# Twenty-four products of a constant on TensorE between two layers of a fused kernel

## The chip, the cores and the metric

The kernel runs on one core of a Trainium2 chip. A core has five engines with a queue of instructions each: TensorE (PE; its weight loads are listed as PEld), VectorE (DVE), ScalarE (ACT), GpSimd (POOL) and SyncE (SP), which here only issues transfers. An engine takes its instructions in the order of its queue and waits on semaphores for the others. The metric is the device time of one execution in microseconds, as the median of several runs.

## The reference

Two transformer layers over 8 sequences of 256 tokens with 256 features, all in float32:

```python
x = x + attention_0(layernorm(x))      # softmax over rows plus softmax over columns, 16 heads
x = x + experts_0(layernorm(x))        # 4 experts, top 2 of them, and one shared expert for all tokens
x = x + time_mixing_1(layernorm(x))    # RWKV: a recurrence over time, then a norm, a gate and a product
x = x + experts_1(layernorm(x))        # 8 experts, top 2 of them, with biases
```

The shared expert is `(silu(xt @ sw1.T) * (xt @ sw3.T)) @ sw2.T`. The time mixing makes three mixtures of each token with the one before it, multiplies each by a 256x256 matrix (k, v and r), and runs the recurrence over k and v.

## The kernel before

Everything stays in on-chip memory as `xs[b]`, one tile per sequence. The experts work on gathered rows: for each layer the sequences are split in two groups (five and three), so there are four expert objects: `one` and `two` for the first layer, `three` and `four` for the second. Each writes its normed tokens to DRAM (`asked`), chooses and routes them, gathers them back in tiles of 128 rows of one expert each (`xg`, L1002, an indirect transfer issued by POOL), turns each tile on TensorE (L1012), multiplies it by the expert's weights (L1020), and scatters the results (L1050). `combine` adds them to `xs[b]` (L1111).

The handoff between the layers is where the second group still has shared-expert work (`two.shared()`, L941 to L954), the time mixing of earlier sequences is under way, and `three`'s tiles begin. The time mixing of one sequence is ten stages: `norm` (L216 and L217 on POOL, L235 on ScalarE: xr), `mix` (transposes L246, the copy L1151, VectorE's dx L1141 and the mixtures L1159), `project` (24 products L1170, copies L1178 and L1176), `exponents` (L1186, L1141 with d, then L1196 to L1200 on ScalarE), `denominator` (L1209), `invert` (L1217), `numerator` (L1224), `norm_inner` (transposes L1236, statistics L1241), `gate` and `project_out`.

Three things set the order of the work. The generators are woven together in Python (`weave`), which gives the order in which instructions are written down. A planner then places them: it models the time, and at each point takes the ready instruction with the highest precedence, which is the order of writing, changed by `tc.high_priority(offset=n)` (a positive n puts a block ahead, a negative one behind). Third, `tc.issue_after(i)` says that what the block issues on the engine of instruction i must be queued behind i. The result is a fixed queue for each engine. PSUM tiles come from tags with a number of buffers: in this part `mm` has three, `ps` two, `sc` three. The shared expert and the tiles' products (L1020) take theirs from `mm`.

The second layer's expert weights (`v1s`, `v2s`, L1345 to L1347) are fetched during the handoff as well, into the place of the first layer's weights. `ones` is a constant 128x128 tile of float32 that is filled at the start.

The lines that the change follows, at the handoff:

```python
with tc.issue_after(three.routed.ins):
    weave((shared, 4))          # the rest of two.shared()
ctx0.close()
...
weave((back, 3), (take(mixing, 3), 3))
tiles = three.tiles()
weave((take(behind(tiles, 3), 20), 20), (mixing, 15))
```

Of the kernel before, what the change touches and what calls it, by code (L numbers as in the profile page):

```python
# [17 lines left out]
P = 128  # L18
# [25 lines left out]
def weave(*streams):  # L44

    streams = [[g, n, 0] for g, n in streams]
    while streams:
        s = min(streams, key=lambda s: s[2] / s[1])
        s[2] += 1
        try:  # L50
            next(s[0])
        except StopIteration:
            streams.remove(s)
# [7 lines left out]
def take(gen, n):  # L61
    for _ in range(n):
        try:
            next(gen)
        except StopIteration:
            return
        yield
# [3 lines left out]
def two_layers(  # L71
# [26 lines left out]
    nc = tc.nc  # L98
# [25 lines left out]
    def filled(name, value, shape=(P, P)):  # L124
        t = const.tile(list(shape), F32, tag=name, name=name)
        nc.gpsimd.memset(t, value)
        return t

    ones = filled("ones", 1.0)
# [595 lines left out]
    class Experts:  # L725
# [206 lines left out]
        def shared(self):  # L932

            mm = self.mm
            for b in self.seqs:
                xt = self.xts[b]
                pu, pg = mm([P, HS // P, T]), mm([P, HS // P, T])
                for pp, w in ((pu, self.weights[3]), (pg, self.weights[4])):
                    for h in range(HS // P):
                        for c in range(NC):  # L940
                            nc.tensor.matmul(  # L941
                                pp[:, h, :], lhsT=w[:, c, ts(h, P)], rhs=xt[:, c, :], start=(c == 0), stop=(c == NC - 1)
                            )
                s = self.mp.tile([P, HS // P, T], F32, tag="h", name="hs", bufs=3)
                nc.scalar.activation(s, pu, AF.Silu)
                nc.vector.tensor_tensor(s, s, pg, ALU.mult)
                yield
                po = mm([P, TT, D])
                for t in range(TT):
                    for h in range(HS // P):  # L950
                        nc.tensor.matmul(
                            po[:, t, :], lhsT=s[:, h, ts(t, P)], rhs=self.weights[5][:, h, :], start=(h == 0), stop=(h == HS // P - 1)
                        )
                nc.vector.tensor_tensor(xs[b], xs[b], po, ALU.add)  # L954
                yield
# [394 lines left out]
    def layers(is_bounded):  # L1350
# [4 lines left out]
        with ExitStack() as pctx, ExitStack() as ctx0, ExitStack() as actx:  # L1355
# [7 lines left out]
            def bank(tag):  # L1363
                def fresh(shape):
                    return psum["pool"].tile(shape, F32, tag=tag, name=tag, bufs=psum[tag])

                return fresh

            mm, ps, sc = bank("mm"), bank("ps"), bank("sc")
            one, two = (Experts(0, k, w0, lnp, mp, rt, ps, mm, ps) for k in range(2))  # L1370
# [40 lines left out]
            def behind(gen, lag=1):  # L1411

                while True:
                    with tc.issue_after(on_pe[-lag].ins):
                        try:
                            next(gen)
                        except StopIteration:
                            return
                    yield

            steps = two.tiles()
            shared = two.shared()
            tiles = one_by_one(take(steps, 5), take(shared, 1), take(steps, 1), take(shared, 1), steps)
            weave((take(tiles, 1), 1))
            one.spare_tiles()
# [9 lines left out]
            with tc.issue_after(three.routed.ins):  # L1435
                weave((shared, 4))
# [5 lines left out]
            for m in (three, four):  # L1442
                m.weights, m.mp = w1_, mp
            weave((back, 3), (take(mixing, 3), 3))
            tiles = three.tiles()
            weave((take(behind(tiles, 3), 20), 20), (mixing, 15))
            assert four.chosen
# [34 lines left out]
    with tc.If(is_flat > 0) as which:  # L1482
        layers(True)
    with which.Else():
        attention_any()
        layers(False)
# [61 lines left out]
```

## Time and profile before

| | us |
|---|---|
| median of 3 runs (754.13 to 755.09) | 754.26 |
| the profiled execution | 760.07 |
| its span, first to last instruction | 757.7 |
| TensorE busy | 653.3 (86%) |
| VectorE busy | 462.9 (61%) |
| ScalarE busy | 358.8 (47%) |
| POOL busy | 244.5 (32%) |
| mean granted clock of TensorE | 0.941 |

A row of the timeline has the start and the duration in us, the engine, the line of the kernel, the operation with the tile written and the tiles read, the shape, and the number of instructions merged. A bracket at its end gives the idle time of the engine just before the row and what ended it. A row over a stretch of time gives the stretch, its length, TensorE's busy time and instructions in it, the clock granted to TensorE (1.00 is full), the busy share of the DMA engines and GB/s. In the rows by slices the span is cut in 40 equal parts and each digit is a share in tenths. A matmul's duration holds its way through the array, so that in a run of matmuls the next one starts well before the last one ends.

### The profile page before, as it was taken

To read this page: it belongs to the slowest core of one execution; us is meant where nothing else is said; L and a number is where in the kernel's file an instruction comes from. 1 tells how busy PE (TensorE), PEld (TensorE's weight loads), DVE (VectorE), ACT (ScalarE), POOL (GpSimd) and SP (SyncE) were. 2 spreads that over 40 slices of the span, in tenths; PEclk is the share of its full clock that TensorE was granted. 3 is DMA by queue.
4 is the path that set the end of the run, shared out by engine and by line. 5 is a ranking of instruction groups with operands and counts; after the bars stand their busy time and mean duration, and the time that the engine had idled before them with its cause. 6 is when DMAs were issued, how large, how long until landed. Compare 5 with 4: busy or idle time off the path is not lost. (4 is left out here: it accounts for less than half of the span.)

```text
span 757.7 us, 10756 instructions
## 1 busy us (share of the span) xinstructions
PE 653.3 (86%) x3170; PEld 417.3 (55%) x3170; DVE 462.9 (61%) x1216; ACT 358.8 (47%) x761; POOL 244.5 (32%) x319
## 2 busy tenths in 40 slices
PE   3799999996989999998899888986848989989790
PEld 2355555555765666665566656654735656554460
DVE  6699878897351111110866877673998895745542
ACT  3588767772213233322377467544147464423230
POOL 3434333300212333323222132112141446465430
PEclk9699999998999999999999999998879999999996
DMA  7800000001101111112300010002780445556844
GB/s 227 292 1 15 15 15 15 15 15 48 65 15 33 52 36 42 43 41 85 118 29 27 28 39 11 28 29 72 231 283 8 138 126 170 172 194 220 269 127 143
DMA packets 38547, 66.85 MB, mean 88 GB/s; under 512 B 6006, under 2 KB 20654, under 8 KB 38480
## 3 DMA queue, kind: packets, MB, share of 16 engines
q1 hardware_dynamic: 30400, 47.01, 18.9%
q0 software_dynamic: 7392, 18.50, 7.9%
q8 instruction: 31, 0.51, 0.3%
q10 hardware_dynamic: 688, 0.55, 0.2%
q14 instruction: 36, 0.29, 0.1%
HBM read 51.32 MB, written 16.41 MB: 89 GB/s over the span
## 5 line engine op out<-in xcount | busy, mean ns | idle before, releaser
L1002 POOL DMA_INDIRECT xg<-asked,source x77 | 78.4, 1018 | 186.5 <-PE ps L1012 164.1
L1050 POOL DMA_INDIRECT back<-yg,row_i x77 | 80.6, 1047 | 113.7 <-ACT yg L1049 35.3
L1041 DVE TENSOR_TENSOR h<-h,mm 128x512 f32<-128x512 f32 x37 | 25.3, 685 | 108.3 <-PE mm L1020 108.2
L1014 ACT COPY hT<-ps 128x256 f32<-128x256 f32 (+1 forms) x77 | 36.4, 473 | 95.8 <-PE ps L1012 87.2
L1020 PE MATMUL mm<-v1s,xgT 128*128 x160 | 76.9, 600 | 1.5 <-ACT xgT L1014 0.8
L576 ACT ACTIVATE e<-sc,minus 128x512 f32<-128x512 f32 x96 | 59.9, 711 | 28.5 <-PE sc L563 28.4
L1020 PE MATMUL mm<-w2s,hT 128*128 x296 | 72.0, 382 | 0.0
L1020 PE MATMUL mm<-w1s,xgT 128*128 x148 | 71.6, 602 | 0.2 <-ACT xgT L1014 0.2
L1020 PE MATMUL mm<-w3s,xgT 128*128 x148 | 70.7, 597 | 0.0
L577 DVE TENSOR_REDUCE s<-e 128x2 f32<-128x512 f32 x96 | 60.5, 677 | 13.3 <-ACT e L576 13.1
L563 PE MATMUL sc<-qT,kT 32*128 32x512 f32 x256 | 58.1, 703 | 2.9 <-DVE qT L544 2.2
L1020 PEld LDWEIGHTS mm<-w2s,hT 128*128 128x128 f32 x296 | 53.7, 191 | 7.1 <-issue 1.4
L1170 PE MATMUL sc<-mix,rw 128*128 128x256 f32 x192 | 49.3, 405 | 5.9 <-DVE mix L1159 4.2
L515 POOL TENSOR_TENSOR rr<-rr,minus_half 128x32 f32<-128x32 f32 x7 | 38.0, 5429 | 50.0 <-DVE rr L513 49.9
L1012 PEld LDWEIGHTS ps<-ident,h 128*128 128x128 f32 x228 | 28.8, 141 | 44.0 <-issue 27.7
L1020 PE MATMUL mm<-v2s,hT 128*128 x160 | 44.3, 396 | 3.1 <-ACT hT L1014 3.1
L216 POOL TENSOR_TENSOR rs<-mv,eps_ln 128x2 f32<-128x2 f32 x40 | 8.6, 215 | 118.4 <-DVE mv L211 75.6
L1012 PE MATMUL ps<-ident,h 128*128 128x128 f32 x228 | 39.4, 276 | 8.4 <-DVE h L1035 7.2
L1020 PEld LDWEIGHTS mm<-w3s,xgT 128*128 128x128 f32 x148 | 28.0, 193 | 33.9 <-issue 33.2
L1170 PEld LDWEIGHTS sc<-mix,rw 128*128 128x128 f32 x192 | 38.2, 205 | 14.2 <-DVE mix L1159 5.3
L1039 ACT ACTIVATE h<-mm 128x512 f32<-128x512 f32 x37 | 22.1, 598 | 43.1 <-PE mm L1020 43.1
L1032 DVE TENSOR_TENSOR hb<-mm,bias 128x512 f32<-128x512 f32 x40 | 27.5, 687 | 22.5 <-PE mm L1020 18.9
(246 smaller groups left out, 1254.2 us busy)
## 6 DMA issues: line engine op xcount, KB each, us to landing
bias<-bd SPq DMA_DIRECT2D x40, 384.0 KB
y<-back SPq DMA_DIRECT2D x16, 512.0 KB
asked<-xm SPq DMA_DIRECT2D x16, 256.0 KB
x<-in_x_dram SPq DMA_DIRECT2D x8, 256.0 KB
w1s<-in_w_dram SPq DMA_DIRECT2D x4, 512.0 KB
w3s<-in_w_dram SPq DMA_DIRECT2D x4, 512.0 KB
w2s<-in_w_dram SPq DMA_DIRECT2D x4, 512.0 KB
v1s<-in_v1g_dram SPq DMA_DIRECT2D x8, 256.0 KB
```

The costliest lines, as they stand in the source:

```text
L515: on_pool["last"] = nc.gpsimd.tensor_tensor(rr, rr, half, ALU.pow)
L563: nc.tensor.matmul(pa, lhsT=q["kT"][rows, u, ts(t, P)], rhs=q["qT"][rows, u], start=True, stop=True)
L576: nc.scalar.activation(e, pa, AF.Exp, bias=minus)
L577: nc.vector.tensor_reduce(q["s"][:, t, h : h + 2], e, AX.X, ALU.add)
L1002: nc.gpsimd.indirect_dma_start(out=xgs[j], out_offset=None, in_=self.asked, in_offset=bass.IndirectOffsetOnAxis(ap=self.source[:, j : j + ...
L1012: nc.tensor.transpose(pt[:, c, :], src[:, ts(c, P)], ident)
L1014: nc.scalar.copy(to, pt)
L1020: nc.tensor.matmul(po.unsqueeze(1), lhsT=lhsT[:, c, :], rhs=w[:, ds(e, 1), c, :], start=(c == 0), stop=(c == n - 1))
L1032: nc.vector.tensor_tensor(hb, ph, biases[j][:, 0 : 2 * I2], ALU.add)
L1041: nc.vector.tensor_tensor(s, s, pg, ALU.mult)
L1050: inst = nc.gpsimd.indirect_dma_start(out=self.back, out_offset=bass.IndirectOffsetOnAxis(ap=self.row[:, j : j + 1], axis=0), in_=yg, in_o ...
L1170: last = nc.tensor.matmul(po[:, o, :], lhsT=w[:, c, ts(o, P)], rhs=m[:, c, :], start=(c == 0), stop=(c == NC - 1))
```

## The change

It keeps a handle on the last product of the shared expert, and adds a block after the time-mixing steps that follow the weights' issue. The block opens a PSUM tile from tag `mm` and writes 24 products of `ones` with `ones` to it, each overwriting the last. All are to be queued on TensorE behind the last product of `two`'s shared expert, and their precedence is 400 places further back than where they are written. Nothing reads the tile.

```diff
@@ -948,7 +948,7 @@
                 po = mm([P, TT, D])
                 for t in range(TT):
                     for h in range(HS // P):
-                        nc.tensor.matmul(
+                        self.summed = nc.tensor.matmul(
                             po[:, t, :], lhsT=s[:, h, ts(t, P)], rhs=self.weights[5][:, h, :], start=(h == 0), stop=(h == HS // P - 1)
                         )
                 nc.vector.tensor_tensor(xs[b], xs[b], po, ALU.add)
@@ -1442,6 +1442,11 @@
             for m in (three, four):
                 m.weights, m.mp = w1_, mp
             weave((back, 3), (take(mixing, 3), 3))
+
+            with tc.issue_after(two.summed.ins), tc.high_priority(offset=-400):
+                idle = mm([P, P])
+                for _ in range(24):
+                    nc.tensor.matmul(idle, lhsT=ones, rhs=ones, start=True, stop=True)
             tiles = three.tiles()
             weave((take(behind(tiles, 3), 20), 20), (mixing, 15))
             assert four.chosen
```

## The prediction

> **What bounds the kernel now.** I read the page first: TensorE is busy 653.3 us of a span of 757.7 us (86%), so over the whole run it is the fullest engine. But this edit touches one place, and the two rows over the span's 40 slices (18.94 us each) show that this place differs from the average.
>
> ```profile
> PE   3799999996989999998899888986848989989790
> PEclk9699999998999999999999999998879999999996
> ```
>
> Slice 30 (549 to 568 us) has PE at 4 tenths, and the granted clock of slices 28 to 30 falls to 8, 8 and 7 tenths. The chain that ended last is no help: it covers only 740 to 752 us, the last gathers and sums. So I read the timeline of TensorE around 553 us, which is the handoff (the second group's shared expert ends, the third set of tiles begins, the mixing stages run on).
>
> ```profile
> 551.70 1.46 PE L951 MATMUL mm<-sw2s,hs 128*128 128x256 f32 x6
> 553.98 0.44 PE L1012 MATMUL ps<-ident,xg 128*128 128x128 f32 x2 [0.82 <-DMA xg<-asked,source]
> 560.00 0.69 PE L1012 MATMUL ps<-ident,xg 128*128 128x128 f32 x2 [5.58 <-DMA xg<-asked,source]
> 560.48 1.06 PE L246 MATMUL sc<-ident,xr 128*128 128x128 f32 x4
> 561.99 0.66 PE L1012 MATMUL ps<-ident,xg 128*128 128x128 f32 x2 [0.45 <-DMA xg<-asked,source]
> 566.51 8.17 PE L1170 MATMUL sc<-mix,rw 128*128 128x256 f32 x24 [3.86 <-DVE mix L1159]
> 574.52 0.60 PE L1236 MATMUL sc<-ident,num 128*128 128x128 f32 x4
> ```
>
> The shared expert's last product (L951) ends at 553.16. TensorE then waits 0.82 us, works 0.44, waits 5.58 for a gather, works some 2.3 us in pieces, and waits 3.86 for VectorE. The 24 projections of L1170 that follow took 8.17 us; a run of 22 of the same shape at 545.99 us took 5.01. They ran at half clock, as the granted clock says. Rows by stretch, with length, busy us, instructions, clock, DMA share and GB/s:
>
> ```profile
> 421.86:425.27 3.41, 1.50 (x10) 1.00 0.29 100
> 551.57:554.98 3.41, 2.03 (x10) 1.00 1.09 348
> 554.98:558.39 3.41, 0.00 (x0) 1.00 1.08 370
> 558.39:561.81 3.42, 1.54 (x6) 0.50 1.02 347
> 568.63:572.05 3.42, 3.42 (x9) 0.50 0.00 0
> 602.77:606.18 3.41, 1.99 (x9) 1.00 0.57 187
> ```
>
> I cut the span at steps of 3.41 us because the clock's changes at 524.26, 558.39 and 572.05 us are 10 and 4 such steps apart. In this grid the clock fell after the window with nothing in it (554.98), but also after windows with 1.12 us (520.85), 1.42 us (674.45) and 1.50 us of work (421.86, in the fence); it stayed full after windows with 1.99 and 2.03 us. So about 1.5 to 2.0 us of work in each 3.41 us is what keeps the clock.
>
> Who decides when the handoff is over? Not TensorE:
>
> ```profile
> 562.19 0.69 DVE L1141 TENSOR_TENSOR dx<-x 128x512 f32<-128x512 f32 x1 [0.44 <-issue]
> 562.80 3.35 DVE L1217 RECIPROCAL den<-den 128x512 f32<-128x512 f32 x1
> 573.62 0.69 DVE L1141 TENSOR_TENSOR d<-k,pp 128x512 f32<-128x512 f32 x1
> 575.15 0.77 DVE L1241 BATCH_NORM_STATS2 st<-sc 128x6 f32<-128x256 f32 x2 [0.72 <-PE sc L1236]
> ```
>
> ```profile
> 574.34 0.51 ACT L1196 ACTIVATE ex<-d,edecay 128x256 f32<-128x256 f32 x1 [0.77 <-DVE d L1141]
> ```
>
> VectorE has no idle time from 562.19 to 574.4. ScalarE starts its exponents at 574.34 when VectorE's d is done, then runs without a pause to 581.7; TensorE, back at 575.53, waits 0.77 us at 579.98 for a copy queued in that run. A faster TensorE between 566 and 575 only waits longer at 579.98.
>
> **The change part by part.** It keeps a handle on the last product of L951, and adds 24 products of the 128x128 constant ones in f32, into one PSUM tile of tag mm, that nobody reads. Nothing is removed or moved, no DMA is issued, and no engine but TensorE gets work.
>
> *Price of the 24.* The nearest row has the same shape, 128x128 moved over 128x128 in f32: L246 at 574.95, 4 in 0.60 us, one alone 0.27, so a step of 0.11. At full clock 24 cost 23 x 0.11 + 0.27 = 2.8 us. At half clock the row at 560.48 has 4 in 1.06 with one at 0.42, a step of 0.21: 23 x 0.21 + 0.42 = 5.3 us. Those are the two ends for the sum of added work; I take 2.8, as they start at 553.16 on a full clock.
>
> *Where they go.* They may not be issued before L951's last, and with the lowest precedence they go where the planner sees TensorE free. The queue is in order, so what matters is what is queued behind them: the transposes of the first gathered tile (xg, ready at 553.98), of the second (560.00), L246 of xr (560.26), and then L1170. What the planner sees between the first and second gather can be read from the order on POOL:
>
> ```profile
> 553.81 0.19 POOL L216 TENSOR_TENSOR rs<-mv,eps_ln 128x2 f32<-128x2 f32 x1 [4.81 <-DVE mv L211]
> 554.15 0.98 POOL L1002 DMA_INDIRECT xg<-asked,source  x1 [0.15 <-DMA xg<-asked,source]
> 555.15 0.74 POOL L217 TENSOR_TENSOR rs<-rs,minus_half 128x2 f32<-128x2 f32 x1
> ```
>
> The second gather stands behind L216, which needs statistics done at 553.7, about when L951 ends; its own issue takes 1 us and its landing more. So in any sensible model TensorE is free for some 3 us there, and most of the 24 fit between 553.2 and 557.0. If they stand before the first xg's transposes, those slip from 553.98 to about 556.0: their copy on ScalarE runs at 558.74 behind other work, and the buffer is needed by a gather issued at 558.64, so cost nothing. If behind, TensorE is busy to 554.4 + 2.7 = 557.1. Either way 0 of the 2.8 us is on the path. If that cover is gone, each product costs 0.11 to 0.21 us ahead of L246.
>
> *The PSUM tile.* Tag mm has three buffers; L951's last result is read by 554.3, and the next user is L1020 at 575.53. No wait: 0. If the 24 were scattered as far as that, the tiles would have two buffers for a time.
>
> *What the clock makes of it.* The Trainium skill ("TensorE: Matmul & The Clock Gate", Part 1) says that the clock halves after an idle window of about 3.4 us, and its closing table asks for no idle gap above about 3 us. By that rule the edit works: the gap of 5.58 shrinks to about 3.0 (557.1 to 560.0), the next one of 3.86 holds a whole window only at (3.86 - 3.41) / 3.41 = 13% of the phases, and L1170 would mostly run warm, 23 x 0.22 + 0.38 = 5.45 us in place of 8.17, a gain of 2.7 us on TensorE. By this trace's windows it doesn't: a window needs 1.5 to 2.0 us of work. After the edit TensorE is busy to 556 or 557, idle to 560.0, busy some 1.5 us until 562.4, idle to 566. A window that ends between 558.8 and 562.2 then holds at most some 1.5 us, and at every position of the grid one such window exists. The clock falls later, at about 558.4 to 562, and is still low at 566.5. I take the measured windows: gain on L1170 0 us, with 2.7 as the other end.
>
> What is left is the work at 560. If the clock is still full there, the second xg's transposes end in 0.44 in place of 0.69 and L246 in 0.60 in place of 1.06: about 0.6 us, of which VectorE can use the 0.44 it stands idle before dx. This needs a favourable position of the grid, some half of them: about 0.2 us.
>
> *Sum:* 0 (products) + 0 (buffer) + 0 (L1170) - 0.2 = -0.2 us, against the profiled execution: 757.7 - 0.2 = 757.5 of span, 760.07 - 0.2 = 759.9 in all. That execution is 5.8 us above the median of the runs, and I carry the difference over: 754.26 - 0.2 = **754.1 us**.
>
> **The rivals.** *Slower: part of the products land behind the second xg.* The planner doesn't know that the gather lands only at 560.0, under the weights' transfer (DMA share 1.07 there). Each product that it puts between these transposes and L246 then runs at half clock ahead of L246, 0.21 us each, and dx, the reciprocal, mix and L1170 come that much later, on a VectorE with no slack. From 7 products on it is over 1.5 us; ten give 2.1 (756.4), all 24 give 5.2, **759.4 us**. For it: the gather's order, and 2.8 us of products into a gap of perhaps 3. Against it: one has to assume that the planner's gap is short.
>
> *Slower by a changed order.* The whole order is worked out by the planner, and a product in progress can hold up a real one and flip an order far behind it. Its price is that of a bubble like the one at 604.7 to 606.9 us (2.1 us of TensorE waiting for ScalarE's xm): one more gives **756.4**, two 758.5. For it: hundreds of instructions after 553 us are placed by small differences. Against it: they are low in rank and over before the mixing goes on.
>
> *Faster: the clock holds, or comes back earlier.* If L1170 runs warm and all of its 2.7 us reach the end, **751.5 us**. For it: the skill's rule; and L1241 waits 0.72 us for TensorE. Against it: the windows, and ScalarE's row at 574.34, after which TensorE waits anyway; without a change of order I see no more than 0.44 + 0.72 = 1.2 us.
>
> *It does nothing at all*, the products lie in the gap and the clock is as before: 754.3, in my own case.
>
> **How the numbers follow.** What a measurement of this kernel can tell from no change is about 0.2%, 1.5 us. No visible change: 0.44, its own range 752.8 to 755.7. Products in the way: 0.20. Changed order: 0.14. Faster: 0.22. So faster 0.22, same 0.44, slower 0.34. The range reaches to the full gain below (751.5) and to the full price of 24 cold products above (759.5); what lies outside is a larger change of order, 2 in 10 at most.
>
> **What would show it.** Right: a group of 24 products on the new line, all between 553 and 558 us, mean 0.27; L246 of xr still at about 560.3; the clock at half when L1170 starts; L1170's 24 in 7 to 8 us; ScalarE's L1196 within 0.5 us of where it was relative to that gather. Wrong: products after 560 and L246 late; L1170 at 5.5 us and the stages behind it earlier by as much; or the order of tiles and mixing different from 575 us on, which no step here can price.

## The result and the profile after

The change made the kernel slower. The median of 13 runs is 758.49 us, against 755.47 us for the kernel before in 13 runs: ratio 1.0053, interval 1.0028 to 1.0077, some 4 us. This ratio, like all below, leaves out runs more than 1.5% above the fastest of the same kernel (here one of the kernel before, 763.12 us); the medians of all runs by themselves give 1.0040, 3 us. The prediction said 754.1 us and "no visible change" as the likeliest case. Single runs of either kernel scatter over 10 to 15 us, and the profiled execution of the changed kernel happens to be its shortest (754.34 us, span 752.0). So I don't compare the two spans, but stretches inside them.

Read first the timeline of TensorE through the handoff in the changed kernel. Time zero for the comparison is the end of the shared expert's last product (L951): 553.16 us before, 549.09 after. L1449 is the new line.

```profile
547.63 1.46 PE L951 MATMUL mm<-sw2s,hs 128*128 128x256 f32 x6
548.92 2.39 PE L1449 MATMUL mm<-ones 128*128 128x128 f32 x20
551.16 0.38 PE L1012 MATMUL ps<-ident,xg 128*128 128x128 f32 x2
551.37 0.39 PE L1449 MATMUL mm<-ones 128*128 128x128 f32 x2
555.90 0.69 PE L1012 MATMUL ps<-ident,xg 128*128 128x128 f32 x2 [4.14 <-DMA xg<-asked,source]
556.38 3.19 PE L1449 MATMUL mm<-ones 128*128 128x128 f32 x14
559.37 0.42 PE L246 MATMUL sc<-ident,xr 128*128 128x128 f32 x1
559.58 0.63 PE L1449 MATMUL mm<-ones 128*128 128x128 f32 x2
560.01 0.85 PE L246 MATMUL sc<-ident,xr 128*128 128x128 f32 x3
560.65 0.63 PE L1012 MATMUL ps<-ident,xg 128*128 128x128 f32 x2
561.07 1.37 PE L1449 MATMUL mm<-ones 128*128 128x128 f32 x10
565.82 8.23 PE L1170 MATMUL sc<-mix,rw 128*128 128x256 f32 x24 [3.38 <-DVE mix L1159]
```

Two things are to be seen. The 24 products are 48 records: a product of 128x128 in f32 appears as two records. And 16 of these records, eight products, stand behind the second gathered tile's transposes and ahead of, or among, the four transposes of xr. The second tile's transposes, which wait for its gather, began 6.8 us after L951's end in both kernels. From there to the end of xr's transposes it took 1.54 us before (560.00 to 561.54) and 4.96 after (555.90 to 560.86): 3.42 us more, 0.43 for each of the eight.

VectorE and ScalarE pass it on. First VectorE, then ScalarE, in the changed kernel:

```profile
556.99 0.68 DVE L1141 TENSOR_TENSOR den<-den,ex 128x512 f32<-128x512 f32 x1
561.51 0.69 DVE L1141 TENSOR_TENSOR dx<-x 128x512 f32<-128x512 f32 x1 [3.84 <-ACT x L1151]
562.12 3.35 DVE L1217 RECIPROCAL den<-den 128x512 f32<-128x512 f32 x1
614.99 3.34 DVE L1217 RECIPROCAL den<-den 128x512 f32<-128x512 f32 x1
```

```profile
573.65 0.51 ACT L1196 ACTIVATE ex<-d,edecay 128x256 f32<-128x256 f32 x1 [0.70 <-DVE d L1141]
```

VectorE's wait ahead of dx is 3.84 us in place of 0.44, 3.40 more. From dx to ScalarE's L1196 it is 12.14 us after and 12.15 before. From dx to the last reciprocal of the mixing, which before is this row, it is 53.5 us in both:

```profile
615.68 3.35 DVE L1217 RECIPROCAL den<-den 128x512 f32<-128x512 f32 x1
```

So the 3.4 us are carried over the 53.5 us behind dx without any being given back, and they agree with the 4 us of the comparison within its interval. That they arrive at the kernel's end is told by the runs alone: the stretch from that reciprocal to the end scatters by more than 3.4 us (142.0 us before, 137.0 after, and see the repeats below). The queues of the other four engines are the same in both kernels, instruction for instruction as far as the profile lists them; only TensorE's differs, and only at this place.

### The profile page after: what moved, and what is told of

Read it like the earlier page. It is cut to its first block, busy times and chain, and to the rows that moved or that the text cites. A ratio compares the mean times of both kernels' runs of the same rounds, so it can differ in the third digit from the quotient of the medians.

```text
span 752.0 us, 10852 instructions
## 1 busy us (share of the span) xinstructions
PE 652.3 (87%) x3218; PEld 419.0 (56%) x3218; DVE 462.6 (62%) x1216; ACT 359.1 (48%) x761; POOL 244.1 (32%) x319
## 5 line engine op out<-in xcount | busy, mean ns | idle before, releaser
L1170 PE MATMUL sc<-mix,rw 128*128 128x256 f32 x192 | 48.4, 399 | 5.5 <-DVE mix L1159 5.5
L1170 PEld LDWEIGHTS sc<-mix,rw 128*128 128x128 f32 x192 | 37.1, 200 | 13.4 <-DVE mix L1159 6.6
L1020 PE MATMUL mm<-v2s,hT 128*128 x160 | 42.3, 383 | 1.1 <-ACT xgT L1014 0.6
L1020 PEld LDWEIGHTS mm<-v1s,xgT 128*128 128x128 f32 x160 | 27.3, 190 | 22.0 <-issue 18.9
```

The lines of the kernel that those rows point to most:

```text
L1020: nc.tensor.matmul(po.unsqueeze(1), lhsT=lhsT[:, c, :], rhs=w[:, ds(e, 1), c, :], start=(c == 0), stop=(c == n - 1))
L1170: last = nc.tensor.matmul(po[:, o, :], lhsT=w[:, c, ts(o, P)], rhs=m[:, c, :], start=(c == 0), stop=(c == NC - 1))
```

## The experiments

The theory after the result: **what stands between the second gather and xr's transposes is paid in full, since VectorE has no slack behind dx.** Rivals: filler work costs by its number wherever it stands; the last five products hold up L1170; the third PSUM buffer of mm is missed; the half clock of L1170 is on the path. In each kernel below the 24 products of the change are replaced as the diff shows, and where nothing else is said, VectorE's and ScalarE's queues are those of the kernel before.

### Ten products

```diff
-                for _ in range(24):
+                for _ in range(10):
```

> Ten f32 products in place of 24; all ten stand ahead of the first gathered tile's transposes, and the queues of the other engines are as before but for one norm instruction on POOL. Theory 'in the way' (the 8 products between the second gather and xr's transposes make the loss): none of the ten is in the way, so ratio to before 1.000 (0.998 to 1.002), and VectorE's wait ahead of dx about 0.4 us as before. Rival 'any filler work at the handoff costs in proportion to its number': 10/24 of 4 us, 1.7 us, ratio 1.002.

Measured: ratio 1.0032 (1.0006 to 1.0058; medians of all runs 1.0011), where 1.000 was expected, and VectorE's wait ahead of dx 2.14 us, where 0.4 was. My theory in its first form (only products are in the way) missed. TensorE's timeline of this kernel shows why:

```profile
559.56 0.38 PE L1012 MATMUL ps<-ident,xg 128*128 128x128 f32 x2
564.31 0.69 PE L1012 MATMUL ps<-ident,xg 128*128 128x128 f32 x2 [4.37 <-DMA xg<-asked,source]
566.48 1.09 PE L246 MATMUL sc<-ident,xr 128*128 128x128 f32 x4 [1.49 <-issue]
```

No product is in the way, yet TensorE stands idle for 1.49 us ahead of L246, for "issue", which means that it waits for nothing that the profile shows. The rows of TensorE's sequencer do show it. In the kernel before, five loads of an expert's number into TensorE's registers (L1027) ran 4.0 to 0.5 us ahead of L951's end, beside products that TensorE was still working off. The products have a higher precedence than these loads (400 places back is not the end of the order), so loads slid behind them. With ten products, three ran between the second tile's transposes and xr's. First the five of the kernel before, from 548 to 553 us, then these three, from 564 to 567 us (duration in ns: least, median, most; then the first and the last start):

```profile
L1027 PEldq TENSOR_LOAD <-whose x5: 296/299/309, 549.1 to 552.0; - x5
```

```profile
L1027 PEldq TENSOR_LOAD <-whose x3: 296/296/305, 564.3 to 565.7; - x3
L1027 PEldq FUSED_REGOPS  x3: 146/146/146, 564.7 to 566.1; - x3
L1027 PEldq SEQ_ASSERT  x3: 18/18/18, 564.9 to 566.3; - x3
```

One load takes 0.30 + 0.15 + 0.02 us on the sequencer, some 0.7 from the start of one to the start of the next, and none of it counts as busy.

### Nineteen products, and the changed kernel again

```diff
-                for _ in range(24):
+                for _ in range(19):
```

> Nineteen f32 products: the same queue as with 24, 10 + 1 + 7 + 1, but without the five behind the third gathered tile. In the way: the same 8 products, so the same loss as with 24, ratio 1.0045 (1.002 to 1.007), VectorE's wait ahead of dx about 3.8 us. Rival 'number': 19/24 of the loss, 1.0042, not told apart by this run alone. Rival 'the last five hold up the projections L1170 behind them': ratio 1.000 to 1.002.

> The changed kernel again on this chip, for comparison in the same batch. Both theories: ratio 1.003 to 1.008; VectorE's wait ahead of dx 3.8 us where the second gather lands some 7 us after the shared expert's last product; less where the gather lands earlier.

Measured with 19: wait ahead of dx 3.86 us, ratio 1.0040 (1.0015 to 1.0066). With 24 in the same batch: wait 3.85 us, ratio 1.0069 (1.0035 to 1.0104). The five products behind the third tile change nothing that the handoff shows: L1170 starts 16.82 us after L951's end with 19, and 16.74 with 24. So these five don't hold up L1170.

### Thirty-six shorter products

```diff
-                for _ in range(24):
-                    nc.tensor.matmul(idle, lhsT=ones, rhs=ones, start=True, stop=True)
+                for _ in range(36):
+                    nc.tensor.matmul(idle, lhsT=lane_h, rhs=lane_h, start=True, stop=True)
```

> 36 products of a bf16 constant in place of 24 of an f32 one, more products but each a quarter to a half of the time; all 36 stand ahead of the second gathered tile's transposes, none in the way of xr's, and the queues of the other engines are as before. 'In the way': ratio 1.000 (0.998 to 1.002), VectorE's wait ahead of dx at most 0.5 us. 'Number': 36/24 of the loss, ratio 1.008.

Measured: ratio 1.0047 (1.0019 to 1.0076), wait ahead of dx 2.92 us. Neither forecast was met: it was too slow for "nothing in the way", too fast for "by number". Four register loads stand there this time, and TensorE's idle time for "issue" ahead of L246 is 2.17 us.

### Eleven products ahead of everything: register loads alone in the way

```diff
-            with tc.issue_after(two.summed.ins), tc.high_priority(offset=-400):
+            with tc.issue_after(two.summed.ins), tc.high_priority(offset=3000):
...
-                for _ in range(24):
+                for _ in range(11):
```

> Eleven f32 products at the highest precedence: they stand right behind the shared expert's last product, then both gathered tiles' transposes, then five loads of expert numbers into TensorE's registers (L1027), which in the kernel before stood ahead of the transposes, then xr's transposes. No product is in the way of xr's; every other engine's queue is as before. Theory 'what now stands between the second gather and xr's transposes is paid, product or register load': a load takes 0.30 + 0.15 + 0.02 us on TensorE's sequencer, some 0.54 with its gaps by the waits of 1.49 us for three and 2.17 for four in the runs with ten and with 36 products; five cost 2.7, VectorE's wait ahead of dx 3.0 to 3.4 us in place of 0.44, ratio 1.0035 (1.001 to 1.006). Rival 'only products are paid': wait 0.4 us, ratio 1.000.

Measured: wait ahead of dx 3.61 us, ratio 1.0057 (1.0027 to 1.0087). TensorE's timeline:

```profile
551.46 2.62 PE L1449 MATMUL mm<-ones 128*128 128x128 f32 x22
553.91 0.38 PE L1012 MATMUL ps<-ident,xg 128*128 128x128 f32 x2
558.52 0.69 PE L1012 MATMUL ps<-ident,xg 128*128 128x128 f32 x2 [4.23 <-DMA xg<-asked,source]
562.08 1.09 PE L246 MATMUL sc<-ident,xr 128*128 128x128 f32 x4 [2.87 <-issue]
```

All eleven products lie in the wait for the gather and cost nothing. The five loads behind the second tile cost TensorE 2.87 us of idle time, and dx is 3.17 us later than before. So a register load can be paid just as a product is, and three, four and five of them gave 1.49, 2.17 and 2.87 us: about 0.7 for each further one. The first of them overlaps the second tile's transposes.

### Five and ten products behind the loads

```diff
-            with tc.issue_after(two.summed.ins), tc.high_priority(offset=-400):
+            with tc.issue_after(two.summed.ins), tc.high_priority(offset=-3000):
...
-                for _ in range(24):
+                for _ in range(5):
```

> Five f32 products at a precedence below the register loads: the five loads stand first as before, then 4 products, the first tile's transposes, 1 product, the second's, xr's. Nothing new is in the way. 'Paid by what stands in between': VectorE's wait ahead of dx 0.3 to 0.5 us, ratio 1.000 (0.998 to 1.002). Rival 'any filler at the handoff, or the third PSUM buffer of mm taken, costs': wait over 1 us or ratio 1.003 and more.

With this precedence the products come behind the loads: the five loads come first again, and no product stands behind the second tile. TensorE, then VectorE:

```profile
555.74 1.05 PE L1449 MATMUL mm<-ones 128*128 128x128 f32 x8
557.10 0.39 PE L1449 MATMUL mm<-ones 128*128 128x128 f32 x2
562.73 0.69 PE L1012 MATMUL ps<-ident,xg 128*128 128x128 f32 x2 [5.24 <-DMA xg<-asked,source]
563.21 1.06 PE L246 MATMUL sc<-ident,xr 128*128 128x128 f32 x4
```

```profile
564.92 0.69 DVE L1141 TENSOR_TENSOR dx<-x 128x512 f32<-128x512 f32 x1 [0.42 <-ACT x L1151]
```

Wait ahead of dx 0.42 us, and from L951's end to dx 9.02 us against 9.03 before. Nothing is in the way, and the handoff is the one of the kernel before. Ratio 0.9972 (0.9949 to 0.9995), of which more below. With `range(10)`:

> As the run with five, with ten products: the added five all stand between the second tile's transposes and xr's. 'Paid by what stands in between': 5 products of two passes at half clock, 5 x 0.43 = 2.1 us, so VectorE's wait ahead of dx 2.6 us, ratio 1.0028 (1.000 to 1.005). Rival 'number': twice the loss of the run with five.

The wait ahead of dx is 2.62 us (2.6 expected), ratio 1.0026 (1.0003 to 1.0049). TensorE's timeline and VectorE's dx:

```profile
562.45 0.69 PE L1012 MATMUL ps<-ident,xg 128*128 128x128 f32 x2 [5.51 <-DMA xg<-asked,source]
562.93 2.34 PE L1449 MATMUL mm<-ones 128*128 128x128 f32 x10
565.06 1.06 PE L246 MATMUL sc<-ident,xr 128*128 128x128 f32 x4
566.78 0.69 DVE L1141 TENSOR_TENSOR dx<-x 128x512 f32<-128x512 f32 x1 [2.62 <-ACT x L1151]
```

Five products in the way, 10 records, move L246 from 0.48 to 2.61 us behind the second tile: 2.13 us, 0.43 each, as in the changed kernel. Filler in general and the buffer are excluded as causes of the handoff's delay by the pair: five products at the same place and with the same buffer cost nothing, and the next five cost 2.2 us of dx.

### All products first, and both gaps filled

In the first kernel all 24 have `offset=3000`. In the second, besides, 16 more follow the transposes of xr for the seventh sequence; `hook` holds the last of these transposes and the PSUM tile (cut to the lines of the new block):

```diff
...
+            if b == 6:
+                with tc.issue_after(hook["turned"].ins), tc.high_priority(offset=-400):
+                    for _ in range(16):
+                        nc.tensor.matmul(hook["idle"], lhsT=ones, rhs=ones, start=True, stop=True)
...
```

> All 24 f32 products at the highest precedence, right behind the shared expert's last product (24 x 0.22 = 5.3 us at full clock), then xr's transposes, then the gathered tiles'. The order of later work differs from before in some 60 places on TensorE and 50 on VectorE. Theory: no wait of VectorE for dx at all (0 in place of 0.44 us). For the clock: by the measured windows (under 1.5 us of work in 3.41 us lets it fall), it is still full at xr's transposes (0.60 us in place of 1.06) but half again when L1170 starts, whose 24 take 7 to 8.2 us; by the rule of an idle window it stays full, 5.5 us. Ratio 0.999 by the first, 0.996 to 0.999 by the second, both open to what the changed order adds, up to 1.004.

> 24 f32 products at the highest precedence right behind the shared expert's last product, and 16 more behind xr's transposes, one ahead of the third gathered tile and 15 behind it, to hold or bring back the clock ahead of L1170. Nothing is ahead of xr's transposes that waits. The order of later work differs from before in some 150 places on TensorE. If the clock is full for most of L1170, its 24 take 5.5 to 6.5 us in place of 8.17. Theory 'VectorE sets the handoff's end': ScalarE's first exponent L1196 stays 12.1 us behind dx, as in every run so far, however long L1170 takes; ratio 1.000 plus what the changed order adds (0.997 to 1.005). Rival 'the cold projections are on the path': L1196 comes up to 2.7 us earlier behind dx, ratio 0.996.

The first: ratio 0.9992 (0.9965 to 1.0019), no wait ahead of dx. Its TensorE by windows of 3.41 us, cut where its clock changes, and the last row of its timeline ahead of the change:

```profile
555.16:558.57 3.41, 3.41 (x32) 1.00 1.07 377
558.57:561.98 3.41, 1.62 (x11) 1.00 1.01 360
561.98:565.39 3.41, 0.59 (x2) 0.50 0.55 193
568.81:572.22 3.41, 3.41 (x9) 0.50 0.00 0
```

```profile
561.93 0.64 PE L1012 MATMUL ps<-ident,xg 128*128 128x128 f32 x2 [1.39 <-DMA xg<-asked,source]
```

The clock was full at xr's transposes, as the prediction hoped for, and fell at about 562.0, after a window with 1.62 us of work, nearly all of it transposes, in which TensorE was never idle for longer than 1.39 us. L1170 then took 8.13 us. That is the measured-windows forecast, and not the one of an idle window. The 0.44 us that a faster L246 could bring were not seen: the planner had put another VectorE instruction ahead of dx, which took 0.60 us.

The second got what the change may have been after. Its TensorE timeline, where L1156 is the 16 products and L1175 the projections (L1170 before):

```profile
558.14 4.68 PE L1156 MATMUL mm<-ones 128*128 128x128 f32 x30
562.66 5.35 PE L1175 MATMUL sc<-mix,rw 128*128 128x256 f32 x24
```

The 24 projections took 5.35 us in place of 8.1 to 8.2. The ratio is 1.0121 (1.0087 to 1.0155), the slowest of all and outside every forecast. dx came 9.08 us after L951's end, as before, but from dx to the end of the kernel it took 201.0 us, against 189.2 to 195.5 in all the other profiles, so the loss lies there. Six register loads now stand ahead of the tiles' first product, which shows 3.61 us of idle time for "issue", and the order of later work differs on all engines. How the loss is made up I have not traced.

L1196 came 11.14 us behind dx, where 12.1 was expected. That is not the full clock's doing as far as the trace tells: in the first kernel, whose L1170 was cold, it was 11.54, since 0.60 us of VectorE's work had moved ahead of dx; in the second VectorE's order changed further, and in both ScalarE still waits for VectorE's d there. As the order of VectorE differs, this run doesn't settle by itself what a full clock in L1170 is worth. The others do, since they share one VectorE order up to L1196: L1170 took 6.92 us with 36 short products, 7.04, 7.31, and 7.84 to 8.23 in the rest, depending on where the clock changed, and from dx to L1196 it was 12.14 to 12.20 us in every one of them. So 1.3 us of L1170 are worth nothing at L1196. Nor do they show later: in the three kernels with the shortest L1170 the last reciprocal came 53.8 to 54.1 us behind dx, in the rest 53.5.

### The five products twice more, and the kernel before against itself

> The kernel with five products behind the register loads again, on another chip or at another time. Its handoff in the trace was that of the kernel before to 0.03 us, so its ratio of 0.997 should not come back: 1.000 (0.998 to 1.002). If it is again 0.997 or less, some gain lies outside the handoff, and the theory lacks a part.

> The kernel before against itself: ratio 1.000, and its distance from 1 shows what the comparison can tell (0.998 to 1.002). In the trace: VectorE's wait ahead of dx 0.4 to 1.0 us, 17.8 to 18.4 us from the dx before it, as in the first profile; the stretch from the last reciprocal of the mixing to the end, 142.0 us in the first profile and 135.7 to 138.9 in all others, falls among the others if it is noise, and is again near 142 if the products change something behind the handoff.

> The kernel with five products behind the register loads a third time, in one batch with the kernel before against itself. If the 0.997 of the two batches before is real: 0.995 to 0.999, with the kernel before at 1.000. If it was noise: 0.998 to 1.002. The handoff in the trace as before in both cases.

Five products: 0.9974 (0.9949 to 0.9998) and 0.9980 (0.9958 to 1.0002), after 0.9972. The kernel before against itself: 0.9993 (0.9969 to 1.0018). Three times in a row a quarter of a per cent, 1.5 to 2.1 us, where 1.000 was expected for the second. The medians of all runs say less: 0.9991, 1.0002 and 0.9971. The handoff is the same: dx came 9.02, 9.57 and 9.19 us after L951's end, against 9.03 and 9.67 in two profiles of the kernel before. The stretch from the last reciprocal to the end was 136.0, 138.4 and 138.2 us, against 142.0 and 138.4. The 142.0 did not come back in the repeat, so it is scatter. Whether the kernel with five products gains anything at all is not shown, and no trace here shows where a gain would come from. That stays open.

| between the second tile's and xr's transposes | wait ahead of dx, us | L1170's 24, us | ratio | medians of all runs |
|---|---|---|---|---|
| nothing (before, two profiles) | 0.44, 1.09 | 8.17, 7.87 | 0.9993 | 0.9992 |
| nothing (5 products elsewhere, three) | 0.42, 0.97, 0.61 | 8.14, 7.84, 8.09 | 0.9972, 0.9974, 0.9980 | 0.9991, 1.0002, 0.9971 |
| 3 loads (10 products elsewhere) | 2.14 | 7.31 | 1.0032 | 1.0011 |
| 5 products (5 elsewhere) | 2.62 | 7.04 | 1.0026 | 1.0025 |
| 4 loads (36 short products elsewhere) | 2.92 | 6.92 | 1.0047 | 1.0026 |
| 5 loads (11 products elsewhere) | 3.61 | 8.22 | 1.0057 | 1.0052 |
| 8 products (11 elsewhere) | 3.86 | 8.12 | 1.0040 | 1.0027 |
| 8 products (16 elsewhere, the change) | 3.84, 3.85 | 8.23, 8.18 | 1.0053, 1.0069 | 1.0040, 1.0067 |

The waits tell the rows apart. The ratios, with intervals of some 0.0025 to either side, tell the ends of the table apart, but not one row from the next.

## Why the prediction was wrong, step by step

**What bounds the handoff: right.** VectorE's chain from dx sets its end. In every kernel with VectorE's order unchanged, each microsecond by which dx was late arrived at L1196, and the ratios rise with it, as closely as their intervals allow.

**The price of a product: wrong by a factor of two.** I took it from L246, "the same shape, 128x128 moved over 128x128 in f32", a step of 0.11 us. But L246 is a transpose, which has one record each. A product in f32 has two: 0.22 us at full clock, 0.43 at half. The profile of before said so, had I counted. L951 has 64 records, and the code makes 8 x 2 x 2 = 32 products:

```profile
L951 PE MATMUL mm<-sw2s,hs x64: 379/379/483, 195.9 to 552.8; 128*128 128x256 f32 x64
```

So 24 products are 5.3 us at full clock, not 2.8.

**Where they go: this is the step that failed.** I wrote that TensorE is free "for some 3 us" in the planner's model and that "most of the 24 fit between 553.2 and 557.0". The planner put ten ahead of the first tile and one ahead of the second, 2.4 us at 0.22 each, so its gap was not much shorter than I had it; then eight stood in the way, and five behind the third tile. With the right price the sum would have warned of the loss: a gap of 3 us holds some 13 products, and up to 11 remain, which ahead of L246 at 0.43 us each are up to 4.7 us. The prediction had this as its rival "products in the way", with a chance of 0.20, at 0.21 each and over 1.5 us "from 7 products on" (its 5.2 us for all 24 should be 5.0 at that price). The mechanism and the place were right; the count of eight at 0.43 gives the 3.4 us.

**What else stood in the queue: overlooked.** The sum spoke of transposes and of the projections L1170 behind the new block, not of the register loads, which count nowhere as busy. In the change they do no harm: four of them ran beside xr's transposes and the products behind, and no idle time for "issue" stands there. In the variants with ten and 36 products they made the whole loss.

**The clock: right about L1170, by another path, and with too simple a limit.** By the rule of the Trainium skill ("TensorE: Matmul & The Clock Gate", Part 1), which asks for an idle window, the edit was to keep L1170 warm. It was cold, 8.23 us. The clock of the changed kernel:

```profile
551.05:554.46 3.41, 0.71 (x7) 1.00 1.09 380
554.46:557.87 3.41, 1.97 (x9) 0.50 1.01 376
557.87:561.28 3.41, 3.41 (x18) 0.50 0.39 134
561.28:564.70 3.42, 1.16 (x10) 1.00 0.15 38
564.70:568.11 3.41, 2.29 (x5) 0.50 0.02 5
```

It fell after a window with 0.71 us of work, was full again after a window of full work at half clock, which the misplaced products had helped to fill, and fell again after one with 1.16 us. The prediction had a single fall, and a clock still low at L1170. Neither window was idle throughout: the longest idle stretch inside was 2.7 us in the first and 2.2 us in the second.

The limit of 1.5 to 2.0 us of work that the prediction read from the first profile is not the whole rule, though. It left out two falls of that profile, at about 104.4 and 162.5 us in the first layer, after windows in which TensorE was busy throughout. The first of them:

```profile
101.02:104.43 3.41, 3.41 (x16) 1.00 0.00 0
104.43:107.85 3.42, 3.42 (x26) 0.50 0.02 5
```

Elsewhere, windows with 1.4 us of work left the clock full (with 19 products at 364.8 us, 1.41), and one with 2.18 us let it fall (with both gaps filled, at 553.8). So neither an idle window nor the busy time alone decides it; what does stays open.

**A full clock in L1170 is worth nothing here: right** as far as the runs with VectorE's order unchanged can show it, that is for 1.3 us of the 2.7. The run with both gaps filled had the full clock there and was slower as a whole, for reasons that are not traced.

**The PSUM buffer at no cost: right**, by the handoff of the runs with five products.

## What to carry to other kernels

Filler work on an engine with a queue in order is free only up to the next instruction that somebody waits for. A planner can put filler behind the wait for a transfer, as this one did, where it is paid in full. So cap the count by what fits ahead of the first such wait, or tie the critical instruction ahead of the filler. Before pricing an instruction from a neighbour of the same shape, divide the records of a known line by the products that its code makes. And when an instruction is put in front of others, look for the ones that count as idle, such as register loads: what ran hidden beside queued work becomes visible, as idle time for "issue", when it slides behind a wait.

## What the runs showed of the hardware

At full clock an f32 product of 128x128 took two records of 0.11 us, an f32 transpose of the same shape one of 0.11, and a bf16 product (the run with 36) one of 0.056. A load of a number into TensorE's registers took 0.47 us on its sequencer, some 0.7 from one to the next, and appears in no busy time; three, four and five in a row held the queue for 1.49, 2.17 and 2.87 us.

The clock halved after a window of 3.41 us with 1.62 us of work and no idle gap above 1.39 us (all products first, at 562.0), and in the kernel before after a window that was busy throughout (at 104.4).

The scatter of single runs, 10 to 15 us, is partly this clock's. The stretch from the first to the sixth dx has the same instructions in each kernel, and took 172.6 to 172.9, 173.9 to 174.1 or 175.4 to 175.7 us, in three groups. In the first profile of the kernel before, in the last group, the clock was at half from about 367.3 to 370.7 and again from 425.3 to 428.7 us. All six profiles of the last group have both of these falls, at places up to 6 us later, the three of the middle group only the second, up to 5 us earlier, and the five of the first group neither. The rest of the scatter, up to the first dx and at the end, I have not looked into.
